# Sharing single-row fetches between SyncE and ScalarE in turns of five and three, in a recommender kernel

## The chip, the core and the metric

The kernel runs on one core of one Trainium2 chip. A core has TensorE (PE, matmuls; PEld are its weight loads), VectorE (DVE), ScalarE (ACT), GpSimd (POOL) and SyncE (SP), which work side by side and wait for each other through semaphores; 16 DMA engines move data between HBM and the on-chip memory. SP, ACT and POOL can each start transfers from their own queue. The metric is the device time of one execution in microseconds (us). Before the change it is 5021.99 us (median of three runs, 5021.95 to 5024.2).

## The reference, cut to what matters

The reference is a wide-and-deep recommender for 16384 examples (the shapes of the inputs, not the unused constant B, set the batch). For each example 32 rows of 300 floats are averaged out of a table of 50000, three bags of 20 rows and four single rows come from small tables, and the joined vector goes through a small network.

```python
tok = word_emb[token_idx].mean(axis=1)        # [16384, 32] rows of [50000, 300]
e1 = emb_mh1[mh1_idx].mean(axis=1)            # 20 rows of 64 each; e2, e3 alike
o1 = emb_oh1[oh1_idx]                         # o2, o3, o4 alike
emb = jnp.concatenate([tok, e1, e2, e3, o1, o2, o3, o4], axis=1)
wide = (wide_mh1[mh1_idx].sum(axis=(1, 2)) + ... + wide_oh4[oh4_idx][:, 0])[:, None]
h = jax.nn.relu(emb @ W1 + b1)                # 748 -> 1024
h = jax.nn.relu(h @ W2 + b2)                  # -> 512
h = jax.nn.relu(h @ W3 + b3)                  # -> 256
return jax.nn.sigmoid(h @ Wd + bd + wide)
```

## The kernel before, in words

The 16384 examples are 128 tiles of 128, one example per partition. The program is one long loop over steps, eleven to a tile (`STEPS`), in an order written out by hand for PE, DVE, ACT and SP (`manual_schedule`); the order in time then follows from semaphores alone.

**Small tables.** They are not gathered. DVE compares indices with a ramp (`hot`, L501), ACT scales one half of that one-hot block in place (L508), PE multiplies one-hot blocks into counts (`pc`, L519), ACT writes the counts out (`cnt`, L522), and PE multiplies counts by the tables (`pg`, L554), which DVE adds up (L544). There are two `hot` buffers and two `pc` buffers. The block for step i+1 is made while the counts of step i run.

**The network.** Tiles are joined in blocks of three (towards the end two, then one). Its matmuls (L677) are strewn between the steps at a pace; ACT evicts each group with its bias and ReLU (`h`, L688), from two `ph` buffers. The final sigmoid is L726, the store of the outputs follows two steps later.

**Token rows.** Each tile needs 32 rows per example. The rule is an indirect gather on POOL (L337), one instruction per token position, which fetches 128 rows, one into each partition. Two positions make a group; six groups of buffers (`tok_rows`, `TOK_BUFS`) are in turn, and DVE adds a group up three groups later (`TOK_LAG`) with L312, L314 and L319.

Two positions of a tile can be taken off POOL. Position 31 of two tiles in three is fetched by SP with 128 single-row transfers, `fetch(t)`, and position 30 of some tiles by ACT, `ScalarRows`. Such a row needs its offset in a register: the column of 128 indices is loaded from HBM (`load_column`), DVE turns it into byte offsets with two small instructions (`column_offsets`, L370 and L371), then SP loads 32 values at a time, ACT 8, into registers (L375), and each transfer (all of them issued in `hardware_dma`, L161) brings one row of 1200 bytes. The tiles `fetched` and `fetched_scalar` have two buffers each. A position fetched in this way has no gather on POOL.

**Turns.** All transfers of SP and ACT take eight semaphores in turn, called lanes here: transfer k uses lane k mod 8, and in the built program each waits until the transfer before it on its lane has landed. The order in which both engines take lanes is fixed while the program is written. `sync_dma` issues on SP; but when the next lane is one of `SCALAR_LANES`, it first lets `ScalarRows` issue on ACT; only if ACT has no row ready does SP take the lane itself. Before, SP has lanes 0 to 5 and ACT 6 and 7.

**When a fetch runs.** `summed_at(t)` is the step at which tile t's token sum is due. SP's fetch of tile t starts `FETCH_AHEAD` steps earlier and is spread over `FETCH_STEPS` steps. ACT starts at tile `SCALAR_FROM`; at half of a tile's rows it chooses the next tile, the first for which its rows will be there in time at `SCALAR_RATE` rows a step.

Of the kernel before, what the change touches and what calls it, by code (L numbers as in the profile page):

```python
# [19 lines left out]
P = 128  # L20
# [6 lines left out]
TOK_BUFS = 6  # L27
HOT_BUFS = 2
FETCH_FROM = 4
FETCH_STEPS = 16.5  # L30
FETCH_AHEAD = {1: 25.0, 2: 19.5}
COLUMN_AHEAD = 4
COLUMN_LAG = 1
LOADS = 32
LANES = 8
SCALAR_LANES = (6, 7)
SCALAR_FROM = 12
SCALAR_RATE = 2.55
SCALAR_MARGIN = 5.0
SCALAR_LOADS = 8  # L40
SCALAR_WANTED, SCALAR_LEAST = 8, 2
# [43 lines left out]
def kernel(  # L85
# [21 lines left out]
    nc = tc.nc  # L107
# [7 lines left out]
    for f in SMALL:  # L115
        n = -(-tables[f].shape[0] // P)
# [38 lines left out]
    scalar_row = []  # L155

    def hardware_dma(queue, **operands):

        dma = queue.dma_start(**operands)  # L161
        if transfers and transfers[-1][0] is not queue:
            tc.add_manual_dep(
                dma.ins,
                transfers[-1][1],
                mybir.DependencyInfo(mybir.DependencyClass.NoSync, mybir.DependencyReason.DATA),
                reason="the semaphores of transfers are taken in this order",
            )
        transfers.append((queue, dma.ins.name))

    def sync_dma(**operands):

        while len(transfers) % LANES in SCALAR_LANES and scalar_row and scalar_row[0]():
            pass
        hardware_dma(nc.sync, **operands)
# [221 lines left out]
    class ScalarRows:  # L397
# [9 lines left out]
        def choose(self, rows_before):  # L407

            least = self.step + (rows_before + P) / SCALAR_RATE + SCALAR_MARGIN
            t = next((t for t in range(tiles_all) if self.summed_at(t) >= least), None)  # L410
            if t is None or t > tiles_all - 3:
                return None
            return t

# [12 lines left out]

        def __call__(self):

            if self.row == P // 2 and not self.asked or self.row == P and not self.values and self.next_t is None:  # L430
                self.asked = True
                self.next_t = self.choose(P - self.row)
                if self.next_t is not None:
                    load_column(self.next_t, N_TOK - 2, True)
                    self.column_due(self.next_t)
                    return True
            if not self.values:
                return False
            if self.row == P:
                self.t, self.row, self.asked = self.starts.pop(0), 0, False  # L440
                self.rows = fa.tile([P, TOK_D], F32, name="fetched_scalar").bitcast(U8)
            value = self.values.pop(0)
            p = self.row
            hardware_dma(nc.scalar, out=self.rows[p : p + 1, :], in_=word_bytes[:, bass.ds(value, ROW_BYTES)])
            self.row += 1
            self.issued += 1
            if self.row == P:
                fetched[self.t, N_TOK - 2] = self.rows.bitcast(F32)
            return True

    def load_indices(blk):


        b0 = blk * BLOCK
        it = idxp.tile([P, NSUB, N_TOK], I32, name="it")
        sync_dma(
            out=it, in_=idx[b0 : b0 + BLOCK, 0:N_TOK].rearrange("(s p) c -> p s c", p=P)
        )
        ix = keyp.tile([P, 2, N_SMALL], I32, name="ix")
        sync_dma(  # L460
            out=ix, in_=idx[b0 : b0 + BLOCK, IDX_MH:IDX_COLS].rearrange("(p f) c -> p f c", f=2)
        )
        token_indices[blk] = it
        return ix
# [228 lines left out]
    def mlp(block, part=None):  # L693


        n = block.n
        hidden = {}

        def h(name, m, tag):
            def get():  # L700
                if name not in hidden:
                    hidden[name] = hp.tile([P, m, N], F32, name=name, tag=tag)
                return hidden[name]

            return get

        h1, h2, h3 = h("h1", M1, "odd"), h("h2", M2, "even"), h("h3", M3, "odd")
        yield from layer(h1, w1_sb, b1_sb, [block.chunk(k) for k in range(NK)], M1, part)
        yield from layer(h2, w2_sb, b2_sb, [h1()[:, k, 0:n] for k in range(M1)], M2)
        flush_outputs()  # L710
        yield from layer(h3, w3_sb, b3_sb, [h2()[:, k, 0:n] for k in range(M2)], M3)

        def finish():
            po = ps_h.tile([1, N], F32, name="po", tag="ph")
            po = po[:, 0:n].rearrange("o (a b) -> o a b", b=P)
            y = block.wide()
            nc.tensor.matmul(po, ident[0:1, 0:1], y, start=True, stop=False)
            for k in range(M3):
                nc.tensor.matmul(  # L719
                    po,  # L720
                    wd_sb[:, k : k + 1],
                    h3()[:, k, 0:n].rearrange("p (a b) -> p a b", b=P),
                    start=False,
                    stop=(k == M3 - 1),
                )
            nc.scalar.activation(y, po, AF.Sigmoid, bias=bd_sb)  # L726
            b0 = block.first * P

            def store():
                sync_dma(out=out[b0 : b0 + n, :].rearrange("(a b) o -> o a b", b=P), in_=y)  # L730

            stores.append([STORE_LAG, store])

        rows_out.append(finish)
# [63 lines left out]
        n = n_groups * (t + 1) + TOK_LAG  # L798
        return n / FRONT_PACE if n < front else FRONT_STEPS + (n - front) / pace

    fetches = [(summed_at(t) - FETCH_AHEAD[t % 3], t) for t in range(FETCH_FROM, tiles) if t % 3]
    fetching = []

    columns_due = []
# [1 line left out]
    def fetch_rows(step, part):  # L806

        scalar.step, issued = step, scalar.issued  # L810
        if step == scalar_first and not scalar_row:
            scalar_row.append(scalar)
        if part == 1:
            for due, t_s in list(columns_due):
                if step >= due:
                    columns_due.remove((due, t_s))
                    column_offsets(t_s, N_TOK - 2)
                    scalar.ready.add(t_s)
            for at, t_f in fetches:
                if step == int(at) - COLUMN_AHEAD:  # L820
                    load_column(t_f, N_TOK - 1, False)
                if step == int(at) - COLUMN_LAG:
                    column_offsets(t_f, N_TOK - 1)
                if step == int(at):
                    fetching.append((at, Paced(fetch(t_f))))
        for at, rows in list(fetching):
            rows.to(P * (step + part - at) / FETCH_STEPS)
            if step + part - at >= FETCH_STEPS:
                rows.finish()
                fetching.remove((at, rows))  # L830
        if scalar_row:
            scalar.load(scalar.issued == issued)
# [4 lines left out]
        columns_due.append((scalar.step + COLUMN_AHEAD, t))  # L837

    scalar = ScalarRows(summed_at, column_due)
    scalar_first = int(summed_at(SCALAR_FROM) - (P / SCALAR_RATE + 15))  # L840

    def speed(step):
# [154 lines left out]
```

## Time and profile before

| what | value |
|---|---|
| median of the runs | 5021.99 us |
| the profiled execution | 5021.06 us, its span in the trace 5019.3 us |
| PE / DVE / ACT / POOL busy | 4806.3 / 3748.7 / 2726.5 / 3774.2 us |
| gathers on POOL (L337) | 3987, mean 946 ns busy each |
| single rows by SP / by ACT | 10624 (83 tiles) / 3328 (26 tiles) |
| other transfers on SP during the loop | 64 + 64 loads of indices, 83 columns, 52 stores |
| granted clock of TensorE | 0.99 |

In the profile, a row of groups shows the line, engine, operation, tiles and count, then busy time and mean duration of one, then the idle time before it and who ended it. SPq and ACTq are the instructions of a queue (issues of transfers, loads of registers), which do not count as busy time. A row of the waits reads: who waited, for whom, us in total, number of times, longest.

### The profile page before, as it was taken

What the parts mean: (1) busy time and instruction counts of PE and PEld (TensorE: products, weight loads), DVE (VectorE), ACT (ScalarE), POOL (GpSimd) and SP (SyncE); (2) the same over time, 40 slices, a digit from 0 to 9 for tenths busy, and PEclk for the clock granted to TensorE, in tenths of its full rate; (3) what the DMA queues carried; (4) which work ended last, traced back from release to release, by engine and by line L of the source; (5) the groups of instructions that cost most, each with busy time, mean ns of one, the idle gap of its engine ahead of it and who ended that gap; (6) DMA issues with size and microseconds to landing.
All of it is one profiled execution on the core that took longest, in us unless ns stands there. A gap on an engine that the chain in (4) does not pass through costs nothing.

```text
span 5019.3 us, 124363 instructions
## 1 busy us (share of the span) xinstructions
PE 4806.3 (96%) x36356; PEld 3721.3 (74%) x36356; DVE 3748.7 (75%) x6830; ACT 2726.5 (54%) x3658; POOL 3774.2 (75%) x3994
## 2 busy tenths in 40 slices
PE   6799999999999999999999999999999999999999
PEld 4577777777777777777777777667767888888899
DVE  6777777777777777777777777777777777777774
ACT  5455555555555555555555555555555555555552
POOL 7777777777777777777777777777777777777775
PEclk8899999999999999999999999999999999999999
DMA  7444444444444444444444444444444444444443
GB/s 204 127 129 130 129 129 129 129 130 129 129 130 128 129 130 129 130 129 129 129 129 129 130 129 129 130 129 129 130 130 129 129 129 130 130 129 130 129 128 100
DMA packets 291735, 654.13 MB, mean 130 GB/s; under 512 B 147100, under 2 KB 161692, under 8 KB 291048
## 3 DMA queue, kind: packets, MB, share of 16 engines
q0 software_dynamic: 191376, 612.66, 45.1%
q1 hardware_dynamic: 89271, 29.49, 2.7%
q10 hardware_dynamic: 10400, 4.02, 0.4%
q8 instruction: 284, 4.65, 0.4%
q14 instruction: 404, 3.30, 0.2%
HBM read 645.65 MB, written 0.07 MB: 129 GB/s over the span
## 4 chain that ended last, share of the span: by engine, by line
PE 37%; DMA 26%; DVE 15%; issue 12%; POOL 9%; ACT 1%; SPq 1%; ACTq 0%; DVEq 0%; POOLq 0%
DMA tok_rows<-in_word_emb_dram,it 23%; PE ph L677 17%; PE pg L554 14%; POOL tok_rows L337 9%; DVE hot L501 5%; DVE own L319 4%; PE pc L519 4%; DVE own L314 3%; DMA fetched_scalar<-in_word_emb_dram 1%; DMA fetched<-in_word_emb_dram 1%; PE pc L595 1%; DVE g L544 1%; PE po L719 1%; SPq L161 1%; DVE x L599 0%
## 5 line engine op out<-in xcount | busy, mean ns | idle before, releaser
L337 POOL DMA_INDIRECT tok_rows<-in_word_emb_dram,it x3987 | 3773.3, 946 | 1219.3 <-issue 754.1
L508 ACT ACTIVATE hot<-hot 64x768 bf16<-64x768 bf16 (+1 forms) x1408 | 1155.4, 821 | 1820.6 <-DVE hot L501 1664.0
L554 PE MATMUL pg<-terms,cnt 128*128 128x195 bf16 x17664 | 1723.7, 249 | 35.6 <-DVE g L544 35.0
L554 PEld LDWEIGHTS <-cnt 128*128 128x128 fp8e3 x17664 | 1529.2, 98 | 83.1 <-issue 54.4
L677 PE MATMUL ph<-x,w_sb 128*128 128x384 f32 (+5 forms) x4932 | 1473.8, 437 | 16.2 <-ACT h L688 11.9
L501 DVE TENSOR_TENSOR hot<-own,sc 128x1656 bf16<-128x1656 bf16 (+1 forms) x1408 | 1393.7, 990 | 126.7 <-PE pc L519 37.7
L522 ACT ACTIVATE cnt<-pc 128x828 uint16<-128x828 f32 (+1 forms) x1408 | 1186.5, 843 | 181.5 <-PE pc L519 103.2
L319 DVE TENSOR_TENSOR own<-own,tok_rows 128x300 f32<-128x300 f32 x1792 | 857.1, 478 | 513.3 <-DMA tok_rows<-in_word_emb_dram,it 468.5
L677 PE MATMUL ph<-h,w_sb 128*128 128x384 f32 (+2 forms) x4160 | 1225.9, 435 | 14.2 <-ACT h L688 14.0
L314 DVE TENSOR_TENSOR own<-own,tok_rows 128x300 f32<-128x300 f32 x1827 | 873.8, 478 | 271.9 <-DMA tok_rows<-in_word_emb_dram,it 221.0
L677 PEld LDWEIGHTS ph<-x,w_sb 128*128 128x128 f32 (+1 forms) x4932 | 830.8, 191 | 305.7 <-ACT h L688 23.0
L519 PEld LDWEIGHTS <-hot 128*128 128x128 bf16 x8192 | 594.2, 98 | 523.8 <-issue 271.3
L677 PEld LDWEIGHTS ph<-h,w_sb 128*128 128x128 f32 x4160 | 700.6, 191 | 266.1 <-ACT h L688 27.3
L519 PE MATMUL pc<-hot 128*128 128x138 bf16 x8192 | 733.1, 225 | 111.8 <-ACT hot L508 51.7
L688 ACT ACTIVATE h<-ph,b_sb 128x384 f32<-128x384 f32 (+2 forms) x723 | 378.7, 524 | 210.5 <-PE ph L677 115.4
L544 DVE TENSOR_REDUCE g<-pg 128x130 f32<-128x390 f32 (+1 forms) x512 | 259.2, 506 | 140.0 <-PE pg L554 138.7
L599 DVE TENSOR_TENSOR x<-pc,scale 128x768 f32<-128x768 f32 x127 | 120.8, 951 | 58.8 <-PE pc L595 57.5
L595 PE MATMUL pc<-ident,g 128*128 128x128 f32 x762 | 107.3, 278 | 5.7 <-ACT cnt L522 5.4
L312 DVE TENSOR_TENSOR own<-tok_rows 128x300 f32<-128x300 f32 x128 | 61.5, 481 | 55.3 <-DMA tok_rows<-in_word_emb_dram,it 52.6
L595 PEld LDWEIGHTS pc<-ident,g 128*128 128x128 f32 x762 | 83.7, 143 | 9.8 <-ACT cnt L522 9.3
L488 DVE COPY sc<-pc 128x512 bf16<-128x512 bf16 x64 | 44.0, 688 | 40.5 <-PE pc L484 39.8
L719 PE MATMUL po<-h,wd_sb 128*1 128x384 f32 (+2 forms) x208 | 67.4, 442 | 4.4 <-ACT h L688 4.4
(59 smaller groups left out, 514.6 us busy)
## 6 DMA issues: line engine op xcount, KB each, us to landing
fetched<-in_word_emb_dram SPq DMA_DIRECT2D x10624, 1.2 KB
tok_rows<-in_word_emb_dram,it POOLq DMA_INDIRECT x3987
fetched_scalar<-in_word_emb_dram ACTq DMA_DIRECT2D x3328, 1.2 KB
ix<-in_idx_dram SPq DMA_DIRECT2D x64, 64.0 KB
w_sb<-in_W_dram SPq DMA_DIRECT2D x6, 512.0 KB
raw<-in_mh_dram SPq DMA_DIRECT2D x4, 682.5 KB
it<-in_idx_dram SPq DMA_DIRECT2D x64, 32.0 KB
w_sb<-in_W_dram SPq DMA_DIRECT2D x1, 2048.0 KB
```

What stands on the lines that cost most here:

```text
L314: nc.vector.tensor_add(tok_sum, tok_sum, a)
L319: nc.vector.tensor_add(to, tok_sum, b)
L337: gather = nc.gpsimd.indirect_dma_start(out=rows[-1], out_offset=None, in_=word, in_offset=bass.IndirectOffsetOnAxis(ap=it[:, j : j + 1], ...
L501: nc.vector.tensor_tensor(hot[:, 0 : 2 * rows, :].rearrange("p i (n d) -> p i n d", d=2), iota.rearrange("p (n d) -> p n d", d=2).unsqueez ...
L508: nc.scalar.activation(upper, upper, AF.Copy, scale=UPPER)
L519: nc.tensor.matmul(pc[:, k // n, at : at + n_h], hot[:, 2 * k, 0:P], hot[:, 2 * k + 1, :], start=True, stop=True)
L522: nc.scalar.activation(cnt[:, :, b : b + rows].rearrange("l h (g k) -> l h g k", g=2), pc[:, :, 0 : n * n_h].rearrange("l g (k h) -> l h g ...
L544: nc.vector.tensor_reduce(field_columns(features(t), pair), pg[:, 0:n, :].rearrange("p f (c d) -> p f d c", c=3), AX.X, ALU.add,)
L554: nc.tensor.matmul(pg[:, j, :], by_slice[:, h, :], terms[:, h, :], start=(h == h0), stop=(h == h1 - 1))
L595: nc.tensor.transpose(pt[:, j // n, j % n, :], g[:, c : c + P], ident)
L677: nc.tensor.matmul(to, weights[: src.shape[0], k, m * P : (m + 1) * P], src, start=(k == 0), stop=(k == len(srcs) - 1),)
L688: nc.scalar.activation(dst()[:, m, 0:n], ph[:, 0:n], AF.Relu, bias=bias[:, m : m + 1])
```

## The change

SP keeps five lanes in eight and ACT gets three. SP fetches position 31 of tiles whose number modulo 8 is 0, 2, 3, 5 or 7, from tile 5 on, each spread over 17.6 steps, with a lead of its own for each residue. ACT starts at tile 8 instead of 12, may go one tile further at the end, and plans with 4.2 rows a step instead of 2.55. Once ACT's rows have begun, the loads of the index tiles `it` and `ix` and the stores of the outputs are put on a list, `scalar_jobs`, from which ACT issues them when its lanes come up; after the last fetch is due, ACT is given no further rows and what is left on the list goes to SP.

In the program as built, SP has 9856 rows (77 tiles), 77 columns and 308 loads of registers; ACT has 5504 rows (43 tiles), 43 columns, 688 loads of registers, 60 + 60 index loads and 49 stores. POOL has 3976 gathers. The order of PE is unchanged; that of ACT's computing instructions too.

```diff
-FETCH_STEPS = 16.5
-FETCH_AHEAD = {1: 25.0, 2: 19.5}
+FETCH_STEPS = 17.6
+FETCH_EVERY = 8
+FETCH_AHEAD = {0: 23.2, 2: 27.6, 3: 21.0, 5: 25.4, 7: 29.8}
-SCALAR_LANES = (6, 7)
-SCALAR_FROM = 12
-SCALAR_RATE = 2.55
+SCALAR_LANES = (5, 6, 7)
+SCALAR_FROM = 8
+SCALAR_RATE = 4.2
...
+    scalar_jobs = []
+
+    def small_dma(**operands):
+
+        if scalar_row:
+            scalar_jobs.append(operands)
+        else:
+            sync_dma(**operands)
...
-            if t is None or t > tiles_all - 3:
+            if t is None or t > tiles_all - 2:
                 return None
...
         def __call__(self):
 
+            if scalar_jobs:
+                hardware_dma(nc.scalar, **scalar_jobs.pop(0))
+                return True
...
-        sync_dma(
+        small_dma(
             out=it, in_=idx[b0 : b0 + BLOCK, 0:N_TOK].rearrange("(s p) c -> p s c", p=P)
         )
...
-                sync_dma(out=out[b0 : b0 + n, :].rearrange("(a b) o -> o a b", b=P), in_=y)
+                small_dma(out=out[b0 : b0 + n, :].rearrange("(a b) o -> o a b", b=P), in_=y)
...
-    fetches = [(summed_at(t) - FETCH_AHEAD[t % 3], t) for t in range(FETCH_FROM, tiles) if t % 3]
+    fetches = [
+        (summed_at(t) - FETCH_AHEAD[t % FETCH_EVERY], t)
+        for t in range(FETCH_FROM, tiles)
+        if t % FETCH_EVERY in FETCH_AHEAD
+    ]
...
+        if step == scalar_last:
+            scalar_row.clear()
+            while scalar_jobs:
+                sync_dma(**scalar_jobs.pop(0))
...
+    scalar_last = int(fetches[-1][0] + FETCH_STEPS)
```

More of the change, by code (lines that the diff above doesn't have):

```diff
@@ L459, in load_indices @@
         ix = keyp.tile([P, 2, N_SMALL], I32, name="ix")
-        sync_dma(
+        small_dma(
             out=ix, in_=idx[b0 : b0 + BLOCK, IDX_MH:IDX_COLS].rearrange("(p f) c -> p f c", f=2)
```

## The prediction

> **What bounds the kernel now.** I began with the page's busy times and groups, where PE is the busiest engine.
>
> ```profile
> span 5019.3 us, 124363 instructions
> PE 4806.3 (96%) x36356; PEld 3721.3 (74%) x36356; DVE 3748.7 (75%) x6830; ACT 2726.5 (54%) x3658; POOL 3774.2 (75%) x3994
> ...
> L337 POOL DMA_INDIRECT tok_rows<-in_word_emb_dram,it x3987 | 3773.3, 946 | 1219.3 <-issue 754.1
> ```
>
> POOL at 75% looks idle, but its gathers plus the idle time before them are 3773.3 + 1219.3 = 4992.6 us, nearly the whole span. So I looked at the gathers one by one, here where they stop longest (timeline of POOL), and at the line's range.
>
> ```profile
> 4926.72 0.95 POOL L337 DMA_INDIRECT tok_rows<-in_word_emb_dram,it  x1 [0.30 <-issue]
> 4927.98 0.94 POOL L337 DMA_INDIRECT tok_rows<-in_word_emb_dram,it  x1 [0.30 <-issue]
> 4929.22 0.95 POOL L337 DMA_INDIRECT tok_rows<-in_word_emb_dram,it  x1 [0.30 <-issue]
> 4932.82 0.94 POOL L337 DMA_INDIRECT tok_rows<-in_word_emb_dram,it  x1 [2.65 <-DVE own L319]
> ```
>
> ```profile
> L337 POOL DMA_INDIRECT tok_rows<-in_word_emb_dram,it x3987: 942/946/1233, 2.8 to 4993.1; - x200
> ```
>
> Every gather comes with the same 0.30 us, whoever is named as releaser; that gap belongs to the gather. One costs (4993.1 - 2.8) / 3986 = 1.252 us from start to start. Adding up what intervals above 1.30 us have over 1.25, I get only 5.4 us in the whole run, 2.35 of them in the last line above. POOL is the bound from its first gather to its last; 5019.3 - 4993.1 = 26 us follow. Two more views say that the others wait for it, and that ACT has room:
>
> ```profile
> ACT hot L508 <- DVE hot L501: 1664.0, 1089, 5.0
> DVE own L319 <- DMA tok_rows<-in_word_emb_dram,it: 468.5, 683, 2.8
> DVE own L314 <- DMA tok_rows<-in_word_emb_dram,it: 221.0, 333, 3.1
> ACT hot L508 <- DMA fetched_scalar<-in_word_emb_dram: 95.1, 92, 3.0
> ACT h L688 <- DMA fetched_scalar<-in_word_emb_dram: 62.9, 84, 1.7
> PE pc L519 <- ACT hot L508: 51.7, 34, 4.0
> ACT cnt L522 <- DMA fetched_scalar<-in_word_emb_dram: 49.8, 67, 1.6
> ```
>
> DVE waits 468.5 + 221.0 + 52.6 (its L312 row) = 742 us for gathered rows. I also took, for each gather, the time from the add that freed its buffers (six groups earlier) to its start: median 9.5 us, never below 4.5 until tile 118, below 1 only in the last nine tiles. So DVE, and PE behind it, may fall some 5 us behind before POOL stops once. The end is POOL's too: the last group is summed 3.4 us after its gather, and the rest is the last tile's network.
>
> **Gathers removed.** SP's tiles fall from 83 to 77, ACT's rise from 26 to 43: 109 positions become 120, and 4096 - 120 = 3976 gathers are left, 11 fewer. 11 x 1.252 = 13.8 us. Here a rule of the Trainium skill speaks against the change: "DMA: Bandwidth & Descriptors", in "Anatomy of one DMA - SWDGE (gpsimd) path", puts dispatch at about 50 ns and generating descriptors at a small cost, the rest being latency that overlaps. By it 11 gathers are worth 11 x 0.05 = 0.6 us and the time stays at 5021.4. The row says 0.946 us busy and 0.30 before it, every time; I take the row.
>
> **SP with five lanes.** A transfer waits for the one eight earlier, so SP's round of lanes cannot be shorter than a landing.
>
> ```profile
> 2270.01 0.58 SPq L161 DMA_DIRECT2D columns<-in_idx_dram  x1
> 2270.69 43.68 SPq L161 DMA_DIRECT2D fetched<-in_word_emb_dram  x110
> ```
>
> ```profile
> L375 SPq TENSOR_LOAD <-columns x332: 2025/2127/2373, 112.1 to 4953.7; - x166
> ```
>
> These 110 rows hold three loads of registers, each 2.13 us and 0.40 around it. (43.68 - 3 x 2.53) / 110 = 0.328 us a row, six of them 1.97 us. From the semaphore records, a row lands 1.93 us after its issue (mean; 1.50 to 2.33 for the middle nine tenths), and the shortest distance between rows is 0.314. So six lanes are just at the landing time. I put the recorded landings through that rule (0.314 after the row before, not before the landing of the row six earlier): 32 rows need 10.76 us; the trace has 10.81. With five lanes the same rule gives 12.42. A fetch then takes 4 x (12.42 + 2.53) + 0.6 for its column = 60.4 us. It may take a fifth of eight tiles: 248.5 gathers x 1.252 = 311 us, 62.2 each. SP is 97% full, where before it needed about 53 of 58.5 us and showed the rest as waits for DVE's offsets (157.4 us on L319 alone). It just fits, because 128 index loads and most of the 52 stores leave it. Those were some 0.5 us each, 0.9 a tile. I cost it at nothing, covered by leads that leave 3.4 to 12.2 steps (12 us or more) between a fetch's planned end and its use. Without that cover, each 1 us over 62.2 would cost up to 77.
>
> **ACT with three lanes.** Added: 2176 rows, 272 loads of registers, 17 columns, 120 index loads, 49 stores. From the timeline of ACT:
>
> ```profile
> 2515.58 0.84 ACT L508 ACTIVATE hot<-hot 64x768 bf16<-64x768 bf16 x1 [3.44 <-DVE hot L501]
> 2515.65 0.53 ACTq L161 DMA_DIRECT2D fetched_scalar<-in_word_emb_dram  x2
> ...
> 2518.07 0.53 ACTq L161 DMA_DIRECT2D fetched_scalar<-in_word_emb_dram  x2
> ...
> 2520.00 0.75 ACTq L161 DMA_DIRECT2D fetched_scalar<-in_word_emb_dram  x2
> ```
>
> A pair is issued while an ACTIVATE runs, and the third pair comes 1.93 us after the second: it waited for the landing, and `hot`, `cnt` and `h` queue behind it. With no overlap at all the addition is 2176 x 0.317 + 272 x 0.76 (ACT's own loads in the trace) + 186 x 0.55 (the price of a column on SP) = 690 + 207 + 102 = 999 us, below the 1664 us in which ACT merely waits for DVE's `hot`. With full overlap it is zero. To it comes lane waiting. The trace has 95 + 63 + 50 = 208 us in 1677 pairs, 0.12 a pair; 1885 threes at that rate make 234 us. At the other end, two threes within a step can cost most of a landing, 0.5 us each or 943 us. I take 0.25, since threes come every 2.4 us on average instead of pairs every 2.7, with a landing of 1.93: 470 us, 262 more. 999 + 262 stays under 1664, so ACT does not become the bound on average.
>
> Single delays count as well. I put ACT's new order through the trace's own times (inputs ready as recorded, rows as above), and the old order too: `hot` ends 0.53 us later on average, `cnt` 0.87. In the trace PE uses a `hot` block 1.8 us (median) after ACT has it, under 0.7 in a tenth of the steps; 12% of the steps would come late, 0.09 us per step averaged over all. PE is idle 2.6% of a step between 1000 and 4000 us, also 0.09 us. That sounds like the edge, but a PE that has once slipped a microsecond meets the next block in time, while POOL has 5 us to give. I take 0 in the long middle. In tiles 123 to 126, where DVE lags POOL by up to 12.8 us and the stop of 2.65 us stands, there is no cover: between 0 (ACT's rows end about there) and 5 us (44 steps of 0.11). I take 1.
>
> **The rest.** ACT's 43 columns and SP's 77 make 11 more pairs of offset instructions on DVE, 22 x 0.22 = 5 us, beside 742 of waiting. The index loads now wait for a lane of ACT, under a step; keys are needed eight steps later, token indices later still. Stores feed nobody. PE's order is the same.
>
> **The sum.** The profiled execution took 5021.06 us, 1.8 outside the span. 5021.06 - 13.8 + 1 = 5008.3. The median of the runs is 0.9 above that execution, so 5009.2; I say 5009.
>
> **Rivals.** (a) ACT becomes what PE waits for; slower. If threes cost 0.5 us or more of lane waiting, ACT has 999 + 735 = 1734 us more to do than before against 1664 it can spare; 70 us too much, and with POOL's gain lost the time is 5022 + 70 = 5090. It decides from about 0.47 us a three. For it: six transfers in a step ask for two landings, 3.9 us, in a step of 3.53. Against: threes are only wanted 1.45 times a step, and part of each hides under ACTIVATEs. (b) SP becomes the bound. If landings average 2.05 instead of 1.93, 32 rows take 13.2 us, a fetch 63.5, and 77 x 1.3 = 100 us have to be made good; less the tightest lead of 12 us and POOL's gain, 5022 + 75 = 5097. It decides at landings of about 2.0. For it: 97% full. Against: eight lanes in all before and after, hence no more transfers in flight. (c) No measurable change: the late tiles or a number of small stops eat 4 us or more of the 13.8; about 5016.
>
> **How the numbers follow.** POOL stays the bound: 0.76, at 5006 to 5012. (c) 0.09. (a) 0.10, (b) 0.05, both mostly slower. About 0.2% (10 us) is what a measurement of this kernel can tell from no change, so faster ends at 5012. Faster 0.77, same 0.08, slower 0.15. The range starts at 5005 (no loss at all, and the present stops shrink by 3) and reaches to 5022, which takes in the first case and (c) and leaves out the slower cases.
>
> **What would show it.** Right: 3976 gathers, still 1.25 us apart, stops of some 6 us in all; SP's waits for DVE's offsets nearly gone, its waits for `fetched` landings up from 132 us to some hundreds; ACT's waits for `fetched_scalar` landings at about twice 208 us, its wait for DVE's `hot` down to about 800; PE idle about the same. Wrong: POOL waiting for DVE's adds in the middle of the run; DVE waiting for `fetched` rows (SP late) or PE's L519 waiting for ACT's `hot` by hundreds of us (ACT late); gathers slower than 1.25 us.

## The result, and the profile after

The change makes the kernel slower. The median of six runs is 5057.05 us (5042.25 to 5065.58), against 5021.22 us for six runs of the kernel before: a ratio of 1.0069, 95% interval 1.0058 to 1.008. The forecast was 5009.0 us, 5005 to 5022. The profiled execution took 5063.97 us, with a span of 5062.2, so it is one of the slower of the six.

First the page after the change: the span, the busy times, and the row of the gathers.

```profile
span 5062.2 us, 127340 instructions
PE 4826.2 (95%) x36356; PEld 3727.6 (74%) x36356; DVE 3777.7 (75%) x6852; ACT 2725.4 (54%) x3658; POOL 3767.3 (74%) x3983
...
L347 POOL DMA_INDIRECT tok_rows<-in_word_emb_dram,it x3976 | 3766.4, 947 | 1264.3 <-issue 828.2
```

The gathers are as many as forecast, 3976, and each is as long as before (947 against 946 ns). Their busy time fell by 6.9 us while the idle time before them rose by 45.0 us, and 0.30 us each of that idle time is the gather's own. Taken as the prediction took it, what the intervals above 1.30 us have over 1.25, the stops add up to 55 us in place of 5.4. POOL's timeline shows one:

```profile
1424.34 0.95 POOL L347 DMA_INDIRECT tok_rows<-in_word_emb_dram,it  x1 [0.30 <-issue]
1425.59 0.95 POOL L347 DMA_INDIRECT tok_rows<-in_word_emb_dram,it  x1 [0.30 <-issue]
1430.80 0.94 POOL L347 DMA_INDIRECT tok_rows<-in_word_emb_dram,it  x1 [4.26 <-DVE own L322]
1432.04 0.95 POOL L347 DMA_INDIRECT tok_rows<-in_word_emb_dram,it  x1 [0.30 <-issue]
```

The last gather now starts at 5031.3 us instead of 4993.1, and about 31 us follow it. So the loss is in POOL's stops, and POOL stops because DVE frees its buffers late. The cover that the prediction found, the time from the add that frees a gather's buffers to its start, was 9.5 us in the median; between groups 100 and 500 it is still 9.1 us, between 1000 and 1500 it is 3.9 us.

The waits after the change (who waited, for whom, us in total, times, longest), with those that answer to the rows shown before and those that are new:

```profile
ACT hot L521 <- DVE hot L514: 703.0, 512, 5.7
DVE g L557 <- PE pg L567: 396.4, 257, 6.7
ACT hot L521 <- DMA fetched_scalar<-in_word_emb_dram: 327.2, 291, 3.1
ACT h L701 <- DMA fetched_scalar<-in_word_emb_dram: 294.7, 320, 2.6
ACT cnt L535 <- DMA fetched_scalar<-in_word_emb_dram: 282.8, 341, 2.8
DVE own L329 <- DMA tok_rows<-in_word_emb_dram,it: 145.3, 217, 3.0
DVE own L324 <- DMA tok_rows<-in_word_emb_dram,it: 72.8, 103, 3.2
PE pc L532 <- ACT hot L521: 64.3, 42, 4.5
DVE columns L380 <- DMA columns<-in_idx_dram: 42.9, 20, 7.0
ACT hot L521 <- DMA fetched<-in_word_emb_dram: 33.2, 9, 7.0
```

DVE waits for gathered rows a third as long as before (145.3 + 72.8 + 17.8 = 236 us instead of 742): it no longer runs ahead of POOL. In their place stand waits for PE's `pg` (396.4 us, before 138.7, in the rows below), and a wait that the trace before did not have: DVE's `columns` (L380) for a column that SP or ACT loads.

Of the kernel before, DVE's wait for `pg` and SP's own waits:

```profile
DVE g L544 <- PE pg L554: 138.7, 114, 4.8
SPq L375 <- DVE own L319: 157.4, 39, 11.6
SPq L161 <- DMA fetched<-in_word_emb_dram: 132.3, 541, 0.6
```

SP's own waits after the change, the durations of its register loads (ns, shortest, median, longest), and its timeline over one fetch:

```profile
SPq L162 <- DMA fetched<-in_word_emb_dram: 662.8, 2138, 1.0
SPq L385 <- DVE own L324: 83.7, 19, 48.2
...
SPq L385 <- DVE own L329: 40.3, 23, 4.0
```

```profile
L385 SPq TENSOR_LOAD <-columns x308: 2032/2129/2335, 152.2 to 4982.5; - x154
```

```profile
1341.77 0.54 SPq L162 DMA_DIRECT2D columns<-in_idx_dram  x1
1342.41 63.58 SPq L162 DMA_DIRECT2D fetched<-in_word_emb_dram  x129
1406.09 0.54 SPq L162 DMA_DIRECT2D columns<-in_idx_dram  x1
```

The rows of L375 and L385 have to be read with care. They count from the end of SP's instruction before, and so take in the 2.13 us of the load itself when a semaphore changes during it; the entries of 1.8 to 2 us after the change are of that kind. Counted in the trace as time in which SP's queue stands idle before a register load (over 0.4 us, from its first row on), SP stopped before 58 of 331 loads in the kernel before, 173.5 us in all and up to 10.6, and before 6 of 307 after the change, 9.6 us in all. So SP is hardly ever early any more; it waits for its own lanes instead, 662.8 us against 132.3. From one column to the next it takes 64.3 us here, where 62.2 are available.

### The profile page after: what moved, and what is told of

It is laid out like the page before. It is cut to its first block, busy times and chain, and to the rows that moved or that the text cites. A ratio compares the mean times of both kernels' runs of the same rounds, so it can differ in the third digit from the quotient of the medians.

```text
span 5062.2 us, 127340 instructions
## 1 busy us (share of the span) xinstructions
PE 4826.2 (95%) x36356; PEld 3727.6 (74%) x36356; DVE 3777.7 (75%) x6852; ACT 2725.4 (54%) x3658; POOL 3767.3 (74%) x3983
## 4 chain that ended last, share of the span: by engine, by line
PE 49%; DMA 27%; DVE 7%; issue 5%; SPq 3%; POOL 3%; ACT 2%; ACTq 2%; DVEq 0%; POOLq 0%
PE ph L690 23%; PE pg L567 18%; DMA fetched<-in_word_emb_dram 11%; DMA fetched_scalar<-in_word_emb_dram 9%; DMA tok_rows<-in_word_emb_dram,it 5%; PE pc L532 5%; DVE hot L514 3%; POOL tok_rows L347 3%; ACTq L162 2%; SPq L385 2%; SPq L162 2%; DVE own L329 2%; DVE own L324 1%; PE pc L608 1%; DMA columns<-in_idx_dram 1%
## 5 line engine op out<-in xcount | busy, mean ns | idle before, releaser
L535 ACT ACTIVATE cnt<-pc 128x828 uint16<-128x828 f32 (+1 forms) x1408 | 1187.6, 843 | 447.3 <-DMA fetched_scalar<-in_word_emb_dram 282.8
L329 DVE TENSOR_TENSOR own<-own,tok_rows 128x300 f32<-128x300 f32 x1792 | 856.7, 478 | 201.5 <-DMA tok_rows<-in_word_emb_dram,it 145.3
L324 DVE TENSOR_TENSOR own<-own,tok_rows 128x300 f32<-128x300 f32 x1823 | 871.9, 478 | 131.6 <-DMA tok_rows<-in_word_emb_dram,it 72.8
L532 PE MATMUL pc<-hot 128*128 128x138 bf16 x8192 | 736.0, 225 | 87.1 <-ACT hot L521 64.3
L701 ACT ACTIVATE h<-ph,b_sb 128x384 f32<-128x384 f32 (+2 forms) x723 | 379.4, 525 | 509.3 <-DMA fetched_scalar<-in_word_emb_dram 294.7
L557 DVE TENSOR_REDUCE g<-pg 128x130 f32<-128x390 f32 (+1 forms) x512 | 260.6, 509 | 399.1 <-PE pg L567 396.4
L608 PE MATMUL pc<-ident,g 128*128 128x128 f32 x762 | 109.2, 281 | 13.1 <-ACT cnt L535 12.8
L322 DVE TENSOR_TENSOR own<-tok_rows 128x300 f32<-128x300 f32 x128 | 61.5, 481 | 21.6 <-DMA tok_rows<-in_word_emb_dram,it 17.8
```

The lines of the kernel that those rows point to most:

```text
L324: nc.vector.tensor_add(tok_sum, tok_sum, a)
L329: nc.vector.tensor_add(to, tok_sum, b)
L532: nc.tensor.matmul(pc[:, k // n, at : at + n_h], hot[:, 2 * k, 0:P], hot[:, 2 * k + 1, :], start=True, stop=True)
L535: nc.scalar.activation(cnt[:, :, b : b + rows].rearrange("l h (g k) -> l h g k", g=2), pc[:, :, 0 : n * n_h].rearrange("l g (k h) -> l h g ...
L557: nc.vector.tensor_reduce(field_columns(features(t), pair), pg[:, 0:n, :].rearrange("p f (c d) -> p f d c", c=3), AX.X, ALU.add,)
L608: nc.tensor.transpose(pt[:, j // n, j % n, :], g[:, c : c + P], ident)
```

## The experiments

Three explanations were weighed. (S) Where ACT has fewer than three rows at hand, SP takes the lane left over; at such a shared turn, ACT's next transfer on that lane waits for a landing of SP's, with ACT's own work queued behind. (B) SP with five lanes is full: it cannot fetch 128 rows in the time of its share, falls behind, and DVE waits for it. (A) ACT's added work (two thirds more single rows, and the loads of indices and the stores) makes `hot`, `cnt` and `h` late for PE.

**Eleven runs give no answer.** The first four kernels, and seven later ones, ran where TensorE was granted 0.87 to 0.88 of its clock on average, instead of 0.99. The kernel before took 7334 to 7418 us there. A profile from there, of the first kernel below:

```profile
PEclk8798888888898888888888898888889889889888
...
POOL tok_rows L347 <- DVE own L329: 2119.2, 602, 12.7
```

The gathers wait 2119 us for DVE instead of 177; they are not the bound there, so neither their number nor a few tens of us of SP's are seen. The edit of the first, e1:

```diff
-SCALAR_WANTED, SCALAR_LEAST = 8, 2
+SCALAR_WANTED, SCALAR_LEAST = 8, 3
```

> The changed kernel, but ACT loads its next eight row addresses when three are left instead of two, so that it always has three rows ready and SP takes none of ACT's lanes in the middle of the run (after: about 45 single turns, nearly all on lane 7). ACT gets one tile more: 3975 gathers. Theory S (in those turns ACT's next transfer waits for a transfer of a late SP, and hot and cnt wait behind it): 5007 to 5015 us, PE-side waits back near those of before. Theory A (threes of rows cost ACT too much lane waiting by themselves): 5045 or more. Theory B (SP with five lanes is full and sets the pace): 5040 or more, since SP's own work is the same.

For e2, SP's column is loaded nine steps ahead of its fetch instead of four:

```diff
+SYNC_COLUMN_AHEAD = 9
...
-                if step == int(at) - COLUMN_AHEAD:
+                if step == int(at) - SYNC_COLUMN_AHEAD:
```

> The changed kernel, but SP loads a tile's column of indices nine steps before its fetch instead of four, so that a late SP does not keep DVE waiting for it; the single shared turns stay (about 40). Theory C (DVE's waits for late columns, 43 us in the profile of after, are the loss): 5010 to 5025. Theory S: 5045 to 5060, the same as after. Theory A: the same as after.

For e3, SP does the index loads and stores again:

```diff
-        if scalar_row:
+        if False:
```

> The changed kernel, but the loads of indices and the stores of outputs stay on SP; ACT gets two tiles more (3974 gathers), the single shared turns are about as many as transfers moved back allow (some 100). Theory J (these transfers on ACT are what costs): 5010 to 5025. Theories B and S: slower than after, 5065 to 5110, since SP has 169 transfers more, about 1 us a fetch, and is later still.

For e4, besides that, the lanes go back to six and two:

```diff
-SCALAR_LANES = (5, 6, 7)
+SCALAR_LANES = (6, 7)
...
-SCALAR_RATE = 4.2
-SCALAR_MARGIN = 5.0
+SCALAR_RATE = 2.25
+SCALAR_MARGIN = 6.0
```

> Only the set of SP's tiles is changed (five in eight over 17.6 steps); lanes are six and two as before, ACT starts at tile 8 with 25 tiles and no other transfers. 3994 gathers, 7 more than before. If the gathers alone set the time: 5022 + 7 x 1.25 = 5031. If the spread or the leads of SP's fetches are at fault (not the lanes): 5050 or more.

Measured for e1 to e4, against 7334.26 us: 7357.6 (ratio 1.0027, interval 1.0015 to 1.004), 7359.03 (1.0027, 1.0015 to 1.0039), 7366.16 (1.0035, 1.0023 to 1.0046) and 7294.02 (0.9925, 0.99 to 0.9951). Nothing is concluded from them on the loss at the full clock; the last one, faster there, is not faster at the full clock, as f3 below shows. Two later sets of kernels met the same low average. They are told with the runs that repeated them.

**No single shared turns: f1.** The edit of e1, at the granted clock of 0.99, called the full clock here (as all that follow unless said otherwise). ACT loads its next offsets as soon as fewer than three are at hand, not two, so it has a row for each of its three lanes, and in the middle of the run no single lane passes between the engines (between 500 and 4500 us SP issued 24 rows on ACT's lanes in the change, none in f1). ACT has 44 tiles, POOL 3975 gathers.

> The kernel of e1_no_shared_turns once more, since e1 to e4 met a chip on which TensorE was granted 0.88 of its clock and the kernel before took 7334 us, so that PE and not the gathers set their time. At a granted clock of 0.99: theory S (ACT waits in single turns for a late SP) 5007 to 5015 us; theory A (threes of rows make ACT late for PE by themselves) and theory B (SP is full) 5040 or more.

Measured: 5085.95 us against 5021.76; 1.0122 (1.0105 to 1.0138). The waits of ACT for SP's landings (33.2 us on `hot` above, 62 us with those on `h` and `cnt`) are gone, and the kernel is another 29 us slower. (S) is not the cause of the loss; SP has also lost the turns that it used to take over, and its fetch is longer (63.4 us for 128 rows instead of 62.9, table below). The profile shows how SP's lateness gets to POOL. The waits, then the timelines of SP, DVE and POOL over the same stretch:

```profile
DVE columns L380 <- DMA columns<-in_idx_dram: 146.0, 42, 7.8
```

```profile
1854.09 64.82 SPq L162 DMA_DIRECT2D fetched<-in_word_emb_dram  x129
1919.22 0.54 SPq L162 DMA_DIRECT2D columns<-in_idx_dram  x1
```

```profile
1914.61 1.01 DVE L514 TENSOR_TENSOR hot<-own,sc 128x1656 bf16<-128x1656 bf16 x1
1922.45 0.21 DVE L380 TENSOR_SCALAR columns<-columns 1x128 int32<-1x128 int32 x1 [6.83 <-DMA columns<-in_idx_dram]
1922.70 0.21 DVE L381 TENSOR_SCALAR columns<-columns 1x128 int32<-1x128 int32 x1
1922.84 0.46 DVE L324 TENSOR_TENSOR own<-own,tok_rows 128x300 f32<-128x300 f32 x1
1923.33 0.48 DVE L329 TENSOR_TENSOR own<-own,tok_rows 128x300 f32<-128x300 f32 x1
```

```profile
1918.90 0.94 POOL L347 DMA_INDIRECT tok_rows<-in_word_emb_dram,it  x1 [0.30 <-issue]
1924.08 0.95 POOL L347 DMA_INDIRECT tok_rows<-in_word_emb_dram,it  x1 [4.23 <-DVE own L329]
```

The next column stands in SP's queue behind rows of the present fetch. SP gets to it at 1919; until it has landed, DVE has waited 6.83 us for it, and the adds queued behind the two offset instructions release POOL 5.2 us after its last gather, not 1.25. A wait of this kind of 3 us and more ends at 1857.1, 1922.4, 1985.3 and 2049.3 us: one per fetch, 63 to 65 us apart. Over this stretch the loop runs at SP's pace.

**And the columns earlier: f2.** The edits of e1 and e2 together. If the column is only badly placed, loading it nine steps ahead ends the loss; if SP is full, DVE waits for something else of SP's.

> f1 and, besides, SP's columns loaded nine steps ahead of a fetch instead of four. Theory S with C (late SP reaches the others through shared turns and through columns, and through nothing else): 5005 to 5012, 3 to 10 below f1. Theory S alone: as f1. Theories A and B: 5040 or more, as f1.

Measured: 5086.67 us; 1.013 (1.0113 to 1.0147). DVE's waits for columns vanish, and in their place it waits for SP's rows:

```profile
DVE own L325 <- DMA fetched<-in_word_emb_dram: 89.7, 13, 14.6
```

The time is unchanged. Where SP's lateness comes out depends on the placing; its size does not.

**Six and two lanes, with the change's tiles for SP: f3.** The edit of e4: SP fetches five tiles in eight, spread as in the change, but has six lanes and the index loads and stores again. ACT has 25 tiles, POOL 3994 gathers.

> The kernel of e4_six_and_two_lanes once more (SP five tiles in eight, lanes six and two, 3994 gathers). At a granted clock of 0.99: if gathers alone set the time, 5022 + 7 x 1.25 = 5031; if the spread of SP's fetches is at fault, 5050 or more.

Measured: 5029.21 us; 1.0016 (1.0009 to 1.0022). SP's waits there:

```profile
SPq L385 <- DVE own L329: 252.2, 31, 38.9
SPq L162 <- DMA fetched<-in_word_emb_dram: 127.8, 521, 0.5
```

SP is early again: it stands idle before 75 of 307 register loads, 407 us in all. POOL's stops are 4.2 us in all, and the time follows from the gathers: 7 more than before, 8.8 us, against 7.5 measured. So the choice of SP's tiles costs nothing; the lanes cost, or the index loads and stores on ACT, on SP's side or ACT's.

**SP's rows not read: k1.** f2 with one more edit: DVE adds a slice of the first weights in place of SP's rows, so that position 31 of 77 tiles is left out of the sum and nobody waits for those rows to land. SP and ACT do all that they did.

```diff
-                        rows.insert(0, fetched.pop((t, j)))
+                        got = fetched.pop((t, j))
+                        rows.insert(0, w1_sb[:, 0, 0:TOK_D] if j == N_TOK - 1 else got)
```

> The kernel of h1 and j1, which both met a chip with TensorE granted 0.87 of its clock: f2, but DVE adds a weight tile in place of SP's rows (position 31 of 77 tiles left out), so that nobody waits for a late row of SP; SP's and ACT's transfers as in f2. At a granted clock of 0.99: theory B (SP with five lanes is full, and its lateness sets the time) 5005 to 5020; theory A (ACT with threes is late for PE, whatever SP does) 5065 or more; between them, both have a part.

Measured: 5061.87 us against 5021.77; 1.0085 (1.0065 to 1.0104). About 25 us of f2's 65 us go; the rest stays. But the edit doesn't free DVE from SP, as was meant:

```profile
DVE columns L382 <- DMA columns<-in_idx_dram: 102.4, 30, 6.5
```

SP's columns are late even though they are loaded nine steps ahead. So the run, which by its number lies near the range that was put down for (A) and far from that for (B), does not part the two. The same kernel at the low average clock, twice:

> f2, but DVE does not read SP's rows: in their place it adds a weight tile that is in the chip already, so position 31 of 77 tiles is left out of the sums. SP's and ACT's transfers and all other work are as in f2; only nobody waits for a late row of SP (in f2 DVE waits 90 us for them). Theory B (SP with five lanes is full, and its lateness sets the time): 5005 to 5020. Theory A (ACT with threes is late for PE, whatever SP does): 5065 or more.

> The kernel of h1 once more, since h1 to i1 met a chip that granted TensorE 0.87 of its clock (before 7418 us). f2, but DVE adds a weight tile in place of SP's rows, so position 31 of 77 tiles is left out and nobody waits for a late row of SP. At a granted clock of 0.99: theory B (SP with five lanes is full, and its lateness sets the time) 5005 to 5020; theory A (ACT with threes is late for PE, whatever SP does) 5065 or more.

It measured 7447.53 us against 7417.98 (1.0043, 1.0031 to 1.0056), and 7437.48 against 7417.45 (1.0027, 1.0016 to 1.0039).

**ACT with a sixteenth of its register loads: k2.** f2, and ACT loads eight offsets once a tile and uses them for all 128 rows, so that position 30 of its tiles gets the rows of eight examples only. It takes 660 of ACT's 704 register loads away and leaves its transfers.

```diff
-            self.values += load_offsets(self.column, self.loaded, SCALAR_LOADS, mybir.EngineType.Activation)
+            if self.loaded == 0:
+                self.kept = list(load_offsets(self.column, 0, SCALAR_LOADS, mybir.EngineType.Activation))
+            self.values += self.kept
```

> The kernel of h2 and j2, which both met a chip with TensorE granted 0.87 of its clock: f2 (5087 us), but ACT loads addresses once a tile and uses the same eight for 128 rows (wrong rows of position 30 in 44 tiles), some 530 us less on ACT's queue; SP, its rows and all who wait for them as in f2. k1 left 40 us of f2's loss when nobody waited for SP. Theory A: ACT's queue carries that, and 5035 to 5065 here. Theory B: 5080 or more.

Measured: 5048.91 us against 5023.45; 1.0058 (1.0047 to 1.0069). That is in the range put down for (A), not in that for (B), and some 39 of f2's 65 us are gone. Between 500 and 4500 us, ACT has some 200 us more than in f2 in which it neither works, issues nor waits for a lane. But the gain is not shown to come to PE by way of ACT's computing: SP is as full as before (it stands idle before 2 register loads), its 128 rows took 62.6 us, against 63.2 in f2 (table below), and 77 fetches of 0.64 us less are 49 us, all of what lies between the two profiled executions (5083.9 and 5034.5; k2's is the fastest of its eight). Why SP's rows land sooner with fewer loads on ACT was not tested. DVE still waits for SP's rows:

```profile
DVE own L325 <- DMA fetched<-in_word_emb_dram: 71.8, 11, 11.6
```

At the low average clock ran the same kernel, its opposite, f3 with one more register load for every second row of ACT's (those rows of position 30 are then those of a tile's first example), and the kernel before with SP fetching seven tiles in ten. They give no answer, and the last two were not repeated at the full clock; so a fuller SP with six lanes, and a busier ACT beside an SP that is not full, stay untested there:

> f2, but ACT loads row addresses into registers once a tile and uses the same eight for all its 128 rows (the rows of position 30 are the wrong ones in 44 tiles): 44 loads instead of 704, some 530 us less on ACT's queue; rows, lanes and SP as in f2. Theory A: 5010 to 5045, since ACT gets half of what it was burdened with back. Theory B: 5075 or more, SP being as late as before.

> f3 (six and two lanes, set by the gathers at 5029), but ACT loads eight addresses anew for every second row: 2000 loads instead of 400, some 1250 us more on ACT's queue, about what after added to it, with no more lanes or rows (the reloaded rows of position 30 are the wrong ones). SP is not full here. Theory A: 5045 or more, ACT's delays reach PE. Theory B: 5028 to 5035.

> The kernel before with lanes six and two, ACT untouched, SP fetching seven tiles in ten over 15.7 steps instead of two in three over 16.5: 87 tiles, ACT 27, 3983 gathers, 4 fewer. SP needs some 55 us a fetch where it has 55.6. If SP keeps up: 5022 - 4 x 1.25 = 5017. If it is full: 5025 to 5060. Theories A and B do not differ here.

> The kernel of h2 once more: f2, but ACT loads addresses once a tile and uses the same eight for 128 rows (wrong rows of position 30 in 44 tiles), some 530 us less on ACT's queue. At a granted clock of 0.99: theory A 5010 to 5045; theory B 5075 or more.

> The kernel of h3 once more: f3 (six and two lanes, 5029 us, set by the gathers), with 2000 loads of addresses on ACT instead of 400 (reloaded rows of position 30 are the wrong ones), some 1250 us more on ACT's queue and no more lanes or rows. At a granted clock of 0.99: theory A 5045 or more; theory B 5028 to 5035.

Measured, in this order: 7431.02 us (1.002, 1.0009 to 1.0031), 7414.99 (1.0001, 0.9986 to 1.0015), 7434.17 (1.003, 1.0015 to 1.0046), each against 7417.98; 7432.7 (1.002, 1.0007 to 1.0032) and 7410.05 (0.9988, 0.9974 to 1.0003) against 7417.45.

**SP with 4% more time, ACT as loaded as in the change: m1.** SP fetches three tiles in five, 75 instead of 77, each spread a little further; five lanes and three, and the jobs on ACT, stay. ACT has 42 tiles, POOL 3979 gathers.

```diff
-FETCH_STEPS = 17.6
-FETCH_EVERY = 8
-FETCH_AHEAD = {0: 23.2, 2: 27.6, 3: 21.0, 5: 25.4, 7: 29.8}
+FETCH_STEPS = 18.3
+FETCH_EVERY = 5
+FETCH_AHEAD = {0: 22.5, 2: 26.2, 4: 29.8}
-SCALAR_RATE = 4.2
+SCALAR_RATE = 4.0
-SCALAR_WANTED, SCALAR_LEAST = 8, 2
+SCALAR_WANTED, SCALAR_LEAST = 8, 3
```

> f1 (lanes five and three, no shared turns), but SP fetches three tiles in five instead of five in eight, each over 18.3 steps instead of 17.6: 75 SP tiles and 42 of ACT, 3979 gathers. SP has 64.8 us a fetch where it has been taking 62.6 to 63.4; ACT's rows a step fall by only 4%. In f1, f2, k1 and k2 SP never was early for DVE. Theory B (SP's fetches set the time, k1 too, by its late columns): 5012 to 5022, SP early again at its loads of registers. Theory A (ACT's load, nearly unchanged): 5050 or more.

Measured: 5028.74 us (5021.6 to 5033.99) against 5021.82; 1.0011 (1.0002 to 1.002). Of f1's 64 us, 57 are gone. SP's waits:

```profile
SPq L162 <- DMA fetched<-in_word_emb_dram: 668.0, 2151, 1.1
SPq L385 <- DVE own L329: 112.3, 28, 11.2
SPq L385 <- DVE hot L514: 63.6, 15, 8.5
```

Its lanes are as slow as in the change (668.0 us), but it is early for DVE again: it stands idle before 52 of 299 register loads, 157 us in all. DVE never waits for a column or row of SP's. ACT's load falls as well, but by 4.5%: 5376 rows instead of f1's 5632. At the prediction's prices (0.317 us a row, 0.76 a load) these 256 rows and 32 loads are an estimated 105 us of ACT's queue; k2 took 660 loads or some 500 us from it for 39 us of time, so by proportion this part is worth some 8 of the 57 us. So (B) is the main cause.

It is not all: 5028.74 is above the 5012 to 5022 that were put down for (B). The gathers alone would give about 5012 us. POOL's stops are 22.9 us; up to 4000 us they are 3.0 in all, from 4000 to 4700 they are 3.3, and 16.5 come after 4700 us, among the last blocks (in the kernel before, 2.6 do). The longest:

```profile
4934.71 0.95 POOL L347 DMA_INDIRECT tok_rows<-in_word_emb_dram,it  x1 [0.30 <-issue]
4940.19 0.94 POOL L347 DMA_INDIRECT tok_rows<-in_word_emb_dram,it  x1 [4.54 <-DVE own L329]
```

**And ACT's rows ending earlier: n1.** m1, with ACT's last tile about 116 instead of 124; 38 tiles of it, 3983 gathers.

```diff
-            if t is None or t > tiles_all - 2:
+            if t is None or t > tiles_all - 12:
```

> Edit: the kernel of m1_three_in_five with ScalarE's rows ending about tile 116 instead of 124 (38 tiles of them instead of 42, 3983 gathers instead of 3979). What is open: m1 kept POOL stops of 22.8 us, 16.5 of them after 4700 us, and ended at 5028.7 where its gathers alone bound it at about 5012. If ScalarE's additions beside the fuller late blocks of PE cause these stops: the gathers' bound is 5012 + 4 x 1.25 = 5017, so 5017 to 5022, with the stops after 4700 us down to a few us. If the stops come from elsewhere (the two-tile and one-tile blocks themselves, which the kernel before also has): they stay near 16 us and the time is 5030 or more.

Measured: 5024.14 us (5020.87 to 5028.55), where the kernel before took 5026.0; 0.9996 (0.9987 to 1.0004). That is above the 5017 to 5022 put down, but in its profile all gathers are 0.1% further apart (1.2519 us against 1.2506 in m1), which is 5 us, and the kernel before was 4 us slower in this set, too. The stops after 4700 us are gone: not one. In all they are 8.1 us. So ACT's late rows cause them. Four gathers fewer than before, 5.0 us, less 2.7 more of stops would be 2.3 us gained; 1.9 were measured, within the uncertainty. One stretch of PE (stretch: us; busy us and number of instructions of PE, PEld, DVE, ACT, POOL; granted clock, DMA share, GB/s), m1 first and n1 second:

```profile
4000.00:4700.00 700.00, 677.96 (x5491) 596.63 (x5490) 531.69 (x956) 386.97 (x538) 527.48 (x557) 1.00 0.49 129
```

```profile
4000.00:4700.00 700.00, 684.65 (x5563) 602.38 (x5562) 534.08 (x958) 392.04 (x544) 527.17 (x557) 1.00 0.48 128
```

ACT's last row is issued at 4914 us in m1 and at 4460 in n1. PE gets through 72 matmuls more in this stretch without them (the kernel before: 5561, as n1), 6.7 us of busy time, while POOL has 557 gathers in both. It is tempting to read that PE loses time here, under POOL's cover, and POOL stops later. That is not shown: at 4000 us PE was 60 matmuls ahead in m1, so at 4700 it is only 12 behind n1, and 12 of the 16.5 us of late stops fall before 4914 us, where m1 still has ACT's rows and n1 has none.

**The runs side by side.** Landing: mean time from a row's issue on SP to its semaphore's event. 128 rows: mean interval of SP's rows times 128, columns and register loads among them. Available: SP's share of the gathers' time. All of the profiled execution, in us.

| kernel | landing | 128 rows | available | SP's last row | POOL's stops | execution |
|---|---|---|---|---|---|---|
| before | 1.932 | 58.5, waits for DVE | 58.5 | 4966 | 5.4 | 5021.1 |
| after | 2.018 | 62.9 | 62.2 | 4998 | 55.0 | 5064.0 |
| f1 | 2.041 | 63.4 | 62.2 | 5040 | 98.2 | 5099.7 |
| f2 | 2.036 | 63.2 | 62.2 | 5024 | 81.6 | 5083.9 |
| f3 | 1.947 | 62.4, waits for DVE | 62.2 | 4962 | 4.2 | 5028.5 |
| k1 | 2.037 | 63.1 | 62.2 | 5012 | 70.5 | 5071.8 |
| k2 | 2.012 | 62.6 | 62.2 | 4974 | 29.9 | 5034.5 |
| m1 | 2.027 | 65.2, waits for DVE | 64.8 | 4978 | 22.9 | 5028.7 |
| n1 | 2.007 | 65.2, waits for DVE | 64.8 | 4976 | 8.1 | 5024.6 |

In the five kernels in which SP hardly ever waits for DVE (2 to 7 idle stops before register loads, at most 18 us in all), the execution ends 60 to 66 us after SP's last row, and their order is that of the 128 rows. In the other four, SP stands idle before 52 to 75 loads, and the end comes 49 to 67 us after its last row.

At the full clock none of the kernels beats the one before by more than can be measured.

## Why the prediction was wrong

**Right.** The bound was read rightly. The number of gathers and their cost stood, 3976 and 1.251 us without the stops. The rule of the Trainium skill against which the row was set ("DMA: Bandwidth & Descriptors", "Anatomy of one DMA - SWDGE (gpsimd) path") would have made 11 gathers worth an estimated 0.6 us; f3, where POOL stops no longer than before, has 7 gathers more and took 7.5 us more, so the row was the right price. What SP would wait for was right in kind: stops for DVE's offsets nearly gone (173.5 us to 9.6), waits for `fetched` landings up from 132 to "some hundreds", 662.8.

**The step that failed: "SP with five lanes".** "It just fits ... I cost it at nothing." The rule behind it was right, that a round of lanes can't be shorter than a landing; the landing that went in was wrong. The recorded 1.93 us were taken as fixed, and they became 2.02. 32 rows take 12.93 us from the first issue to the last, not 12.42, and the landing alone accounts for it: 12.42 x 2.018 / 1.932 = 12.97. A fetch takes 62.9 us, not 60.4, and 62.2 were available. By the prediction's own price for lost cover, 77 x (62.9 - 62.2) = 54 us less the lead of 12 makes 42 us, which on 5009 is 5051; the median is 5057. That is rival (b), which was said to decide "at landings of about 2.0" and given 0.05.

The argument against it was "eight lanes in all before and after, hence no more transfers in flight". But lanes are not transfers. Rows times landing over the span give 13952 x 1.932 / 5019 = 5.4 single rows in flight on average before, and 15360 x 2.018 / 5062 = 6.1 after. The trace before already held the warning. Sorted by how many single rows of SP and ACT are in flight when one of SP's is issued (itself included), landings there average 1.85 us at five or six, 1.95 at seven and 2.03 at eight. 36% of SP's rows were issued at eight before, and 49% after. Had the sum been tried with 2.03 instead of 1.93, it would have given an estimated 12.42 x 2.03 / 1.93 = 13.1 us for 32 rows and 63 for a fetch, over the 62.2.

The slack was also read too large. "About 53 of 58.5 us" left 5.5 for waits for DVE's offsets; the trace has 173.5 / 83 = 2.1 us of such stops a fetch, and index loads and stores, with the gaps before them, some 1.7. A resource 97% full, resting on a time measured while it was less full, should have had most of the chance.

**Where it comes out.** "DVE waiting for `fetched` rows (SP late)" was named as the sign of this. In the change's trace the wait stands on the columns instead, since a column is queued behind the rows of the fetch before it; f2 turns one into the other. The two steps that the prediction priced as instructions, 11 more pairs on DVE, cost 5 us of DVE's time as such and are also where SP's queue stops DVE.

**ACT.** The middle came out as forecast, though two terms were off: its wait for DVE's `hot` is 703 us where "about 800" was forecast, and its waits for its own landings are 327.2 + 294.7 + 282.8 = 905 us, over four times 208 and not twice. That is 0.48 us a three in place of 0.25, just past the 0.47 at which rival (a) was to decide. Yet (a) falls: PE's `pc` waits 64.3 us for `hot`, where it waited 51.7, and m1, with 42 of ACT's tiles and the loads and stores on it, has POOL stopping 3.0 us up to 4000 us. The threshold rested on the 999 us counted "with no overlap at all".

The late tiles were mis-sized: "I take 1", between 0 and 5, for the tiles 123 to 126. POOL's stops are 22.9 us in m1 and 5.4 before, 17.5 more, most of them after 4700 us, and n1 removes the late ones by ending ACT's rows some eight tiles earlier. In the change itself SP's part and ACT's overlap and were not parted; 42 and 17 are more together than the 48 by which it misses the forecast.

**Open.** Why a landing takes longer. More rows in flight is a part: with the averages of the trace before for each number in flight, the numbers after the change give 1.95 us, a third of the rise; the rest stands at equal numbers (2.09 us at eight, 2.03 before). Nor is it shown which way this goes, since slow landings themselves keep more rows in flight, and k2 has as many rows as f2 and 2.012 us instead of 2.036.

## What to carry to other kernels

A queue whose transfers wait for a semaphore of a small set can be no faster than lanes over landing time, and the landing time is not a constant: sort it in the trace by the rows in flight, measure it at the load that it will have, or allow for the 5% seen here. When a change fills a resource to 97%, the slack that the trace shows (here SP's waits for DVE) is what is being spent, and the end then follows that resource's pace; giving it 4% more time (m1) was worth 57 us, while moving the place of the wait (f2) was worth nothing. Before such slack is counted on, make sure that the waits are idle time: a view of waits can take in the waiting instruction's own time. A delay that is covered at first (9.1 us of cover, then 3.9) should be followed to where the cover ends.

## What was not expected of the hardware

At the granted clock of 0.99, single-row landings rose from 1.93 to between 2.01 and 2.04 us in all kernels with five and three lanes, and stayed at 1.95 with six and two (f3), on SP's queue and ACT's alike (2.018 and 2.015 in the change).

In the eleven runs at a mean granted clock of 0.87 to 0.88, the kernel before takes 7334 to 7418 us instead of 5022, 46 to 48% more for 12% less clock, and none of the comparisons made there foretold one at the full clock. The clock is not the whole of it. In e1's trace the records of the granted clock alternate between 0.5 and 1; 294 stretches at 0.5 are 1817 us together (141 us in the change's trace), which can cost PE at most half of that, 909 us, while e1's span is 2261 us longer than that of f1, the same kernel. PE is busy for 5627 of 7359 us there and idle for the rest. Whether the low clock makes PE idle or the idle time lowers the clock is not shown. In these traces SP's single rows land in 1.50 to 1.64 us, with some three in flight on average and DMA moving 88 to 90 GB/s instead of 128 to 130. It is not shown to be a lasting trait of a chip either: k2 ran at the full clock on the chip that the record numbers 13, where h1 to i1 had run at 0.87.

Between the profiles of m1 and n1, on two chips at the full clock, the interval of gathers differed by 0.1% (1.2506 and 1.2519 us), which is 5 us here.
